# Storing less of a masked adjacency: turned parts only, byte masks for the rest

## The chip, the cores and the metric

The kernel runs on one core of a Trainium2 chip. The metric is device time in microseconds of one execution. It is written in Bass with the Tile framework, which sets the semaphores, hands out buffers and orders each engine's instructions. The engines are TensorE (PE, with its weight loads as PEld), VectorE (DVE), ScalarE (ACT), GpSimd (POOL) and SyncE (SP). SP, ACT and POOL issue DMAs.

## The reference

A batch holds 16 graphs of 1024 nodes with 128 features each. `adj` is a weighted adjacency with some 6% of its entries above zero. Its pattern is symmetric, its weights are not. Layer 0 is three graph convolutions, layer 1 a dilation of the adjacency and three more convolutions:

```python
def _sage(x, adj, Wr, Wx, b, mf):
    deg = jnp.clip(jnp.sum(adj, axis=-1, keepdims=True), 1.0, None)
    agg = jnp.einsum('bij,bjd->bid', adj, x) / deg
    out = agg @ Wr + x @ Wx + b
    nrm = jnp.maximum(jnp.linalg.norm(out, axis=-1, keepdims=True), NORM_EPS)
    return out / nrm * mf[..., None]
# layer 0: h = relu(layernorm(x)); three times h = (adj * cos(h W + b)) @ (h W + b); x = x + h
# layer 1: h = relu(layernorm(x))
adj_d = _dilate(adj, mask)          # keeps or drops entries, row after row
h1 = _bn(relu(_sage(h,  adj_d, Wr1, Wx1, b1, mf)), g1, be1)
h2 = _bn(relu(_sage(h1, adj_d, Wr2, Wx2, b2, mf)), g2, be2)
h3 = _bn(relu(_sage(h2, adj_d, Wr3, Wx3, b3, mf)), g3, be3)
xc = jnp.concatenate([h1, h2, h3], axis=-1) * mf[..., None]
return x + (xc @ Wl + bl) * mf[..., None]
```

`_bn` takes its statistics over all batches and nodes, so each convolution of layer 1 ends in a barrier over the 16 batches.

## The kernel before

All matrices are cut into blocks of 128 x 128, eight to a side (NCH = 8). Row q of a batch is handled as one tile of 2 x (8 - q) - 1 blocks: first the 8 - q blocks from the diagonal on, turned (transposed), then the 7 - q blocks of the mirrored column. For all q that makes 64 blocks a batch.

**Layer 0 and the dilation** share the first part. `layer0` is a generator: batches go in pairs, and `order` lists 48 rounds (six for a pair: three convolutions of two batches in turn). In a round, `products` forms cosines on PE and multiplies them into the adjacency on DVE, `turn` transposes, `sums` and `sums_back` accumulate, and line 387 evicts the round's sum into hTo. At fixed steps of a round, other work is placed: `fetch` loads x, `norm` is the layer norm (lines 135 to 150), `residual` and `next_layer` end a batch. Whether the next round is a batch's first is asked by `then.l == 0` and `after.l == 0`; `l` is raised in `sums_back`, three steps late. `adjT_tile` also transposes the adjacency and stores its upper blocks in `adjT_d` (line 242). The dilation runs between these pieces, by a planner's weights (`COLS`, `TURN`, `SPREAD`), mostly on DVE; it stores a 0/1 pattern `keep_d` in f16 (line 716).

**The second layer's first convolution** (block `c1`): `fetch` loads `kb`, the pattern of a batch, and `hN`. `masked(b, q, kb)` loads the turned blocks from `adjT_d` (line 920) and the others from `adj` (line 924) into slot aT{q}, transposes the pattern on PE (929), multiplies the two patterns into `both` (931), and masks the two parts of the slot (937 and 941). `turn` transposes the second part (954, 955) and stores the whole slot to `adT_d` (956, on POOL's queue). `follow`, two steps later (`LAG1`), runs `Sums.add`, whose matmuls (827) read the slot. A slot exists once for each q, so the next batch's loads wait for this batch's matmuls and for its store.

**The second and third convolution** (loop `for l in (1, 2)`): per batch eight loads `aT <- adT` (line 1043, on SP's queue), each followed by `add`. At q = 2 `start2` prepares the next batch: `normed` (1002), `weighted` (PE 799, ACT 800, DVE 801), and `project` (1012), which adds the projection of the previous convolution's output to `acc` (by ACT at 1020 or by DVE at 1022). In the third convolution `residual` loads x2 and adds bias and x2 to `acc` with 16 operations (1030 and 1034). `weigh` (856), `norms` (872, 876, and POOL at 877) and `keep` (165, 166, 887) end the sums. **The tail** projects the last output and adds `acc` (1068).

Tile orders instructions by priority, the order of the program, and moves ready ones into gaps that its model of the engines shows.

Of the kernel before, what the change touches and what calls it, by code (L numbers as in the profile page):

```python
# [7 lines left out]

F32 = mybir.dt.float32
F16 = mybir.dt.float16  # L10
I32 = mybir.dt.int32
AF = mybir.ActivationFunctionType
ALU = mybir.AluOpType
# [24 lines left out]
COLS, TURN = 0.215, 0.109  # L38

LAG1 = 2  # L40

SPREAD = 0.93
T_DIL = 10
# [3 lines left out]
def tile_adj_preln_d2(  # L47
# [49 lines left out]
    def base(q):  # L97


        return q * 2 * NCH - q * q  # L100

    dram = ctx.enter_context(tc.tile_pool(name="dram", bufs=1, space=DRAM))
    keep_d = [dram.tile([N, N], F16, tag=f"keep{b}", name=f"keep{b}") for b in range(B)]
    adT_d = [
        [
            dram.tile([P, base(q + 1) - base(q), P], F32, tag=f"adT{b}_{q}", name=f"adT{b}_{q}")
            for q in range(NCH)
        ]
        for b in range(B)
    ]  # L110
    adjT_d = [dram.tile([NCH, P, N], F32, tag=f"adjT{b}", name=f"adjT{b}") for b in range(B)]
    x2_d = [dram.tile([N, D], F32, tag=f"x2{b}", name=f"x2{b}") for b in range(B)]
    h0_d = [dram.tile([N, D], F32, tag=f"h0{b}", name=f"h0{b}") for b in range(B)]
# [55 lines left out]
    with ExitStack() as actx:  # L169
# [242 lines left out]
        batches = [Batch(b) for b in range(B)]  # L412
        order = [batches[b + i] for b in range(0, B, 2) for _ in range(3) for i in range(2)]

        def layer0():


# [24 lines left out]
            for i, now in enumerate(order + [None]):  # L442
# [5 lines left out]
                for s in range(NCH if now else LAG):  # L448
# [25 lines left out]
                    if ended:  # L474
# [4 lines left out]
                            yield NCH * TURN  # L479
                        if s == 5:  # L480
                            ended.next_layer()
                    if s == 5 and after and after.l == 0:
                        after.fetch()
                    if then:
                        new = then.l == 0
                        if s == 0 and new:
                            then.norm()
                        if s == 3 and new:
                            then.enter(0)
                            then.enter(1)  # L490
# [280 lines left out]
    with ExitStack() as bctx:  # L771
# [10 lines left out]
        def blocks_of(q, nm):  # L782


            return poolr.tile([P, 2 * (NCH - q) - 1, P], F32, tag=f"aT{q}", name=f"aT{q}_{nm}")

        def weighted(l, b, hT, ones):


            nm = f"{l}_{b}"  # L790
            hw = pool2.tile([P, NCH, P + ones], F32, tag="hw", name=f"hw_{nm}")
            if ones:
                nc.gpsimd.memset(hw[:, :, P:], 1.0)
            own = pool2.tile([P, NCH, D], F32, tag="own", name=f"own_{nm}")
            for h in range(NCH // 2):
                two = slice(2 * h, 2 * h + 2)
                pw = ps_sm.tile([P, 2, 2 * P], F32, tag="sm", name=f"pw_{nm}_{h}")
                for i in range(2):
                    nc.tensor.matmul(pw[:, i, :], lhsT=hT[:, 2 * h + i, :], rhs=wrx[:, l, :], start=True, stop=True)  # L799
                nc.scalar.activation(hw[:, two, :P], pw[:, :, :P], AF.Copy)  # L800
                nc.vector.tensor_tensor(  # L801
                    own[:, two, :], pw[:, :, P:], bs[:, l : l + 1, :].to_broadcast([P, 2, P]), ALU.add
                )
            return hw, own
# [84 lines left out]
        def batchnorm(l):  # L889

            mv = pool2.tile([P, 2], F32, tag="bn_mv", name=f"bn_mv_{l}")
            nc.vector.bn_aggr(mv, stats.rearrange("p s x -> p (s x)"))  # L892
            sd = pool2.tile([P, 1], F32, tag="bn_sd", name=f"bn_sd_{l}")
            nc.scalar.activation(sd, mv[:, 1:2], AF.Sqrt, bias=eps_col)
            nc.vector.reciprocal(sd, sd)
            ab = pool2.tile([P, 2], F32, tag="bn_ab", name=f"bn_ab_{l}")
            nc.vector.tensor_tensor(ab[:, 0:1], sd, gcol[:, l : l + 1], ALU.mult)
            mt = pool2.tile([P, 1], F32, tag="bn_mt", name=f"bn_mt_{l}")
            nc.vector.tensor_tensor(mt, mv[:, 0:1], ab[:, 0:1], ALU.mult)
            nc.vector.tensor_tensor(ab[:, 1:2], becol[:, l : l + 1], mt, ALU.subtract)  # L900
            return ab
# [2 lines left out]
        with ExitStack() as c1:  # L904
# [4 lines left out]
            def fetch(b):  # L909
                kb = poolk.tile([P, NCH, N], F16, tag="kb", name=f"kb_{b}")  # L910
                for c in range(NCH):
                    nc.sync.dma_start(kb[:, c, :], keep_d[b][c * P : (c + 1) * P, :])
                hN = pool2.tile([P, NCH, D], F32, tag="hN2", bufs=1, name=f"hN1_{b}")
                nc.scalar.dma_start(hN, h0_d[b].rearrange("(c p) d -> p c d", p=P))
                return kb, hN

            def masked(b, q, kb):
                row = NCH - q
                aT = blocks_of(q, f"1_{b}")
                nc.sync.dma_start(  # L920
# [6 lines left out]
                pk = ps_t.tile([P, NCH, P], F16, tag="pk", name=f"pkb_{b}_{q}")  # L927
                for c in range(row):
                    nc.tensor.transpose(pk[:, c, :], kb[:, q + c, q * P : (q + 1) * P], ident16)
                both = poolk.tile([P, NCH, P], F16, tag="both", name=f"both_{b}_{q}")  # L930
                nc.vector.tensor_tensor(
                    both[:, :row, :],
                    pk[:, :row, :],
                    kb[:, q, q * P :].rearrange("p (c q) -> p c q", q=P),
                    ALU.mult,
                )
                nc.vector.scalar_tensor_tensor(  # L937
                    aT[:, :row, :], aT[:, :row, :], 0.0, both[:, :row, :], ALU.max, ALU.mult
                )
                if row > 1:  # L940
                    nc.vector.scalar_tensor_tensor(
                        aT[:, row:, :], aT[:, row:, :], 0.0, both[:, 1:row, :], ALU.max, ALU.mult
# [3 lines left out]
            def turn(s, q, aT):  # L946

                b, row = s.b, NCH - q
                for c in range(1, row, CPH):
# [3 lines left out]
                    for i in range(n):  # L953
                        nc.tensor.transpose(pt[:, i, :], aT[:, at + i, :], ident)  # L954
                    nc.scalar.activation(aT[:, at : at + n, :], pt[:, :n, :], AF.Copy)  # L955
                nc.gpsimd.dma_start(adT_d[b][q], aT)

            last, behind = None, []

# [11 lines left out]
            for b in range(B):  # L971
                kb, hN = then
                hT = pool2.tile([P, NCH, P], F32, tag="hT2", name=f"hT1_{b}")
                transposed(ps_sm, hT, hN, f"h1{b}")
                now = Sums(0, b, hT, 3, 1, ps_a)
                for q in range(NCH):
                    behind.append((now, q, masked(b, q, kb)))
                    if len(behind) > 1:
                        turn(*behind[-2])
                    if len(behind) > LAG1:  # L980
# [3 lines left out]
                    if q == 4 and last is not None:  # L984
                        last.keep(0)
                        last.keep(1)
                        last = None
            turn(*behind[-1])
            while behind:
                follow()  # L990
# [4 lines left out]

        poolc = bctx.enter_context(tc.tile_pool(name="bc", bufs=1))
        ps_a = bctx.enter_context(tc.tile_pool(name="b_a2", bufs=2, space=PSUM))
        acc = poolc.tile([P, B, NCH, D], F32, name="acc")

        def normed(l, b, ab):  # L1000
            hT = pool2.tile([P, NCH, P], F32, tag="hT2", name=f"hT2_{l}_{b}")
# [5 lines left out]
        def project(l, b, hT):  # L1007

            for h in range(NHALF):
                pp = ps_sm.tile([P, CPH, P], F32, tag="sm", name=f"pp_{l}_{b}_{h}")  # L1010
                for c in range(CPH):
                    nc.tensor.matmul(pp[:, c, :], lhsT=hT[:, h * CPH + c, :], rhs=wl[:, l, :], start=True, stop=True)  # L1012
                yield h, pp, acc[:, b, h * CPH : (h + 1) * CPH, :]

        def start2(l, b):
            hT = normed(l, b, ab)
            got = Sums(l, b, hT, CPH, 0, ps_a)
            for h, pp, a in project(l - 1, b, hT):
                if l == 1:
                    nc.scalar.activation(a, pp, AF.Copy)  # L1020
                else:
                    nc.vector.tensor_tensor(a, pp, a, ALU.add)
            return got

        def residual(b):

            x2 = pool2.tile([P, NCH, D], F32, tag="hN2", bufs=1, name=f"x2f_{b}")
            nc.scalar.dma_start(x2, x2_d[b].rearrange("(c p) d -> p c d", p=P))
            for c in range(NCH):
                nc.vector.scalar_tensor_tensor(  # L1030
                    x2[:, c, :], blb[:, 0, :], mf[:, b, c : c + 1], x2[:, c, :], ALU.mult, ALU.add
                )
                a = acc[:, b, c, :]
                nc.vector.scalar_tensor_tensor(a, a, mf2[:, b, c : c + 1], x2[:, c, :], ALU.mult, ALU.add)

        for l in (1, 2):
            last = None
            then = start2(l, 0)
            for b in range(B):
                now = then  # L1040
                for q in range(NCH):
                    aT = blocks_of(q, f"{l + 1}_{b}")
                    nc.sync.dma_start(aT, adT_d[b][q])
                    now.add(q, aT)
                    if q == 1 and last is not None:
                        last.keep(0)
                    if q == 3 and last is not None:
                        last.keep(1)
                    if q == 2:
                        if b + 1 < B:  # L1050
                            then = start2(l, b + 1)
                        if l == 2:
                            residual(b)
                    if q == CPH - 1:
                        now.norms(0)
                    if q == NCH - 2 and b == B - 1:
                        now.keep(0)
                now.norms(1)
                last = now
            last.keep(1)  # L1060
            ab = batchnorm(l)

        for b in range(B):
            y = pool2.tile([P, NCH, D], F32, tag="o", name=f"y_{b}")
            for h, pp, a in project(2, b, normed(3, b, ab)):
                for c in range(CPH):
                    n = h * CPH + c
                    nc.vector.scalar_tensor_tensor(  # L1068
                        y[:, n, :], pp[:, c, :], mf2[:, b, n : n + 1], a[:, c, :], ALU.mult, ALU.add
                    )  # L1070
            nc.sync.dma_start(out[b].rearrange("(c p) d -> p c d", p=P), y)


# [48 lines left out]
```

## Time and profile before

| what | us |
|---|---|
| median of 3 runs | 2987.47 |
| lowest and highest | 2986.51, 2990.78 |
| the profiled execution | 2990.07 |
| its span, first to last instruction | 2988.3 |
| PE, PEld, DVE busy in it | 2699.3, 2228.7, 1974.3 |
| ACT, POOL busy in it | 1468.3, 449.3 |

The mean granted clock of TensorE is 0.967. The DMA queues moved 593.67 MB, 199 GB/s on average. "Busy" is time in which an engine worked on an instruction; waits, semaphores and the issuing of DMAs by SP are not in it. Matmuls overlap, so a busy PE is not PE at its peak. "DMA share" is the mean busy share of the core's 16 DMA engines. A wait is put down to whatever ended last before the waiting instruction began.

The stages lie in the span thus: layer 0 with the dilation up to about 1748 us, then the first convolution of the second layer up to 2252, the second up to 2592, the third up to 2932, and the tail.

### The profile page before, as it was taken

How to read it: one execution, taken by the hardware profiler on the slowest of the kernel's cores; microseconds unless marked ns; L12 is line 12 of the kernel's file. 1: busy time of each engine (PE TensorE's matmuls, PEld its weight loads, DVE VectorE, ACT ScalarE, POOL GpSimd, SP SyncE). 2: the span in 40 equal slices, each digit the busy share in tenths (PEclk: the TensorE clock that was granted, in tenths of full speed). 3: DMA queues.
4: the chain of work that ended last, by engine and by line, in shares of the span. 5: the costliest groups of instructions: out<-in, count | busy, mean ns of one | idle time of the engine just before them, and what ended most of it. 6: DMA issues, size and time to landing. Idle time of an engine off the chain costs nothing. (4 is left out here: it accounts for less than half of the span.)

```text
span 2988.3 us, 52459 instructions
## 1 busy us (share of the span) xinstructions
PE 2699.3 (90%) x18803; PEld 2228.7 (75%) x18803; DVE 1974.3 (66%) x5233; ACT 1468.3 (49%) x4213; POOL 449.3 (15%) x604
## 2 busy tenths in 40 slices
PE   5999898998989889998999979988898999899996
PEld 3666676666666666666666668888888999899995
DVE  2878778878878788778877446666662333366555
ACT  5867657657546556566455223333333343333333
POOL 2112012011111111121111012212121101010110
PEclk9999999999999999999999989999999999999998
DMA  8446347346356476296351079999995566566763
GB/s 265 157 137 210 109 153 236 91 158 198 103 171 174 116 218 178 80 262 171 89 176 64 3 262 375 361 351 360 361 322 213 195 206 218 177 227 228 246 213 113
DMA packets 399664, 593.67 MB, mean 199 GB/s; under 512 B 85456, under 2 KB 283984, under 8 KB 399392
## 3 DMA queue, kind: packets, MB, share of 16 engines
q1 hardware_dynamic: 326640, 416.89, 44.6%
q0 software_dynamic: 38464, 156.07, 14.4%
q10 hardware_dynamic: 34288, 17.24, 2.0%
q8 instruction: 152, 2.49, 0.3%
q14 instruction: 120, 0.98, 0.1%
HBM read 411.83 MB, written 163.58 MB: 193 GB/s over the span
## 5 line engine op out<-in xcount | busy, mean ns | idle before, releaser
L827 PE MATMUL agg<-hw,aT 128*128 128x128 f32 (+1 forms) x6144 | 754.8, 280 | 9.1 <-DVE aT L937 8.0
L827 PEld LDWEIGHTS agg<-hw,aT 128*128 128x128 f32 x6144 | 726.7, 196 | 13.8 <-DVE aT L937 11.0
L324 PE MATMUL pg<-nhT 128*128 128x512 f32 (+3 forms) x1152 | 459.3, 501 | 64.7 <-DVE ew L336 59.1
L364 PE MATMUL po<-ew,hS 128*128 128x512 f32 (+3 forms) x1152 | 459.5, 502 | 12.5 <-ACT hTo L387 8.5
L336 DVE TENSOR_TENSOR ew<-pg,adjA 128x768 f32<-128x768 f32 (+3 forms) x528 | 423.7, 824 | 4.4 <-DVEq L764 2.9
L378 PE MATMUL po<-ew,hS 128*128 128x128 f32 x2688 | 365.3, 276 | 0.0
L378 PEld LDWEIGHTS po<-ew,hS 128*128 128x128 f32 x2688 | 337.8, 193 | 35.4 <-issue 34.8
L354 ACT ACTIVATE ew<-gt 128x512 f32<-128x512 f32 (+1 forms) x480 | 208.6, 464 | 219.5 <-PE gt L353 216.2
L324 PEld LDWEIGHTS pg<-nhT 128*128 128x128 f32 x1152 | 189.1, 194 | 162.4 <-issue 110.9
L695 DVE TENSOR_TENSOR_SCAN rank<-patt 128x1024 f16<-128x1024 f16 x128 | 292.4, 2294 | 0.7
L364 PEld LDWEIGHTS po<-ew,hS 128*128 128x128 f32 x1152 | 197.2, 195 | 106.2 <-issue 74.6
L353 PEld LDWEIGHTS gt<-ident,ew 128*128 128x128 f32 x1344 | 168.2, 143 | 102.7 <-issue 70.3
L333 DVE TENSOR_TENSOR ew<-pg,adjA 128x128 f32<-128x128 f32 x384 | 106.5, 277 | 170.5 <-PE pg L324 137.8
L353 PE MATMUL gt<-ident,ew 128*128 128x128 f32 x1344 | 211.9, 277 | 5.8 <-ACT ew L354 4.5
L801 DVE TENSOR_TENSOR own<-pw,bs 128x256 f32<-128x256 f32 x192 | 78.8, 423 | 201.7 <-ACT hw L800 201.7
L877 POOL TENSOR_TENSOR o<-o,rn 128x512 f32<-128x512 f32 x96 | 103.9, 1082 | 668.6 <-DVE rn L876 423.7
L799 PE MATMUL pw<-wrx,hT 128*128 128x256 f32 x768 | 181.1, 390 | 10.4 <-ACT hT L1002 9.7
L955 ACT ACTIVATE aT<-pta 128x512 f32<-128x512 f32 (+3 forms) x160 | 70.5, 468 | 216.6 <-PE pta L954 193.5
L856 DVE SCALAR_TENSOR_TENSOR o<-agg,invdeg,own 128x128 f32<-128x128 f32 x384 | 111.5, 343 | 96.4 <-PE agg L827 87.3
L799 PEld LDWEIGHTS pw<-wrx,hT 128*128 128x128 f32 x768 | 146.2, 195 | 33.1 <-ACT hT L1002 10.5
L800 ACT ACTIVATE hw<-pw 128x256 f32<-128x256 f32 x192 | 70.6, 384 | 202.2 <-PE pw L799 149.0
L872 ACT ACTIVATE own<-o 128x128 f32<-128x128 f32 x384 | 115.3, 303 | 96.6 <-DVE o L856 96.6
(161 smaller groups left out, 4101.8 us busy)
## 6 DMA issues: line engine op xcount, KB each, us to landing
an<-in_adj_dram SPq DMA_DIRECT2D x128, 512.0 KB, 4.8
keep<-kp POOLq DMA_DIRECT2D x128, 256.0 KB, 3.6
kb<-keep SPq DMA_DIRECT2D x128, 256.0 KB, 5.7
aT<-adT SPq DMA_DIRECT2D x32, 960.0 KB, 4.7
aT<-adT SPq DMA_DIRECT2D x32, 832.0 KB, 4.6
xb<-in_x_dram SPq DMA_DIRECT2D x47, 512.0 KB, 4.6
aT<-adT SPq DMA_DIRECT2D x32, 704.0 KB, 4.1
aT<-adT SPq DMA_DIRECT2D x32, 576.0 KB, 3.4
```

Of the source, the lines that this page charges most:

```text
L324: nc.tensor.matmul(pg[:, :n, :].rearrange("p c q -> p (c q)"), lhsT=self.nhT[:, q * P : (q + 1) * P], rhs=self.nhT[:, (q + c) * P : (q + c ...
L333: nc.vector.tensor_tensor(ew[:, 0, :], pg[:, 0, :], place[:, 0, :], ALU.mult)
L336: nc.vector.tensor_tensor(both[0][:, :, off, :], pg[:, own:n, :].unsqueeze(1).to_broadcast([P, 2, n - own, P]), both[1][:, :, off, :], ALU ...
L353: nc.tensor.transpose(pt[:, i, :], ew[:, at + i, :], ident)
L354: nc.scalar.activation(ew[:, at : at + n, :], pt[:, :n, :], AF.Copy)
L364: nc.tensor.matmul(self.po[:, c * P : (c + n) * P], lhsT=self.hS[:, q, :], rhs=ew[:, c - q : c - q + n, :].rearrange("p c q -> p (c q)"), ...
L378: nc.tensor.matmul(self.po[:, q * P : (q + 1) * P], lhsT=self.hS[:, q + n, :], rhs=ew[:, NCH - 1 - q + n, :], start=False, stop=closes and ...
L695: nc.vector.tensor_tensor_scan(rank, pt[:, 1 : N + 1], pt[:, 2:], 0.0, ALU.add, ALU.add)
L799: nc.tensor.matmul(pw[:, i, :], lhsT=hT[:, 2 * h + i, :], rhs=wrx[:, l, :], start=True, stop=True)
L827: nc.tensor.matmul(self.place(c), lhsT=aT[:, blk, :], rhs=self.hw[:, source, :], start=source == 0 and c % self.ga == 0, stop=ends(c, source),
L856: nc.vector.scalar_tensor_tensor(self.o[:, c, :], self.place(c)[:, :P], invdeg[:, b, c : c + 1], self.own[:, c, :], ALU.mult, ALU.add,)
L872: nc.scalar.activation(self.own[:, n, :], self.o[:, n, :], AF.Square, accum_out=ss[:, c : c + 1])
```

## The change

In the first convolution the slot's first part (turned adjacency, masked) is no longer stored; only the second part is. The product of the patterns is written as bytes into a tile `masks` of 36 blocks for the whole batch, and stored once a batch to `mask_d`. In the second and third convolution each slot is filled by two loads, the first part from `adjT_d` (not masked) and the second from `adT_d`, six products ahead (`AHEAD`); the masks come in two pieces a batch (q from 0 to 3, and from 4). DVE masks the first part again (`unmasked`), three products ahead (`MASKED`). The sum `acc` is one tile for each batch; x2 is loaded into it at the start, two batches ahead in the second convolution, each projection is multiplied by the squared node mask and added to it, and `bias` adds the bias in the third. In layer 0 the two questions after `l == 0` become a question after the round's number (`first`), so that `fetch` and `norm` run once for a batch; before, they also ran in the first two rounds of a pair.

```diff
+AHEAD, MASKED = 6, 3
...
-            dram.tile([P, base(q + 1) - base(q), P], F32, tag=f"adT{b}_{q}", name=f"adT{b}_{q}")
-            for q in range(NCH)
+            dram.tile([P, NCH - 1 - q, P], F32, tag=f"adT{b}_{q}", name=f"adT{b}_{q}")
+            for q in range(NCH - 1)
...
+    mask_d = [dram.tile([P, NMASK, P], U8, tag=f"mask{b}", name=f"mask{b}") for b in range(B)]
...
+        def first(i):
+
+            return i % 6 < 2
...
-                    if s == 5 and after and after.l == 0:
+                    if s == 5 and after and first(i + 2):
                         after.fetch()
                     if then:
-                        new = then.l == 0
+                        new = first(i + 1)
...
+        def unmasked(aT, q, mask):
+
+            here = aT[:, : NCH - q, :]
+            nc.vector.scalar_tensor_tensor(here, here, 0.0, mask, ALU.max, ALU.mult)
...
-                both = poolk.tile([P, NCH, P], F16, tag="both", name=f"both_{b}_{q}")
+                both = masks[:, mbase(q) : mbase(q + 1), :]
                 nc.vector.tensor_tensor(
-                    both[:, :row, :],
+                    both,
...
-                nc.vector.scalar_tensor_tensor(
-                    aT[:, :row, :], aT[:, :row, :], 0.0, both[:, :row, :], ALU.max, ALU.mult
-                )
+                unmasked(aT, q, both)
...
-                nc.gpsimd.dma_start(adT_d[b][q], aT)
+                if row > 1:
+                    nc.gpsimd.dma_start(adT_d[b][q], aT[:, row:, :])
...
+                masks = poolk.tile([P, NMASK, P], U8, tag="masks", name=f"masks_{b}")
...
+                nc.gpsimd.dma_start(mask_d[b], masks)
...
-        acc = poolc.tile([P, B, NCH, D], F32, name="acc")
+        acc = [poolc.tile([P, NCH, D], F32, name=f"acc{b}") for b in range(B)]
...
+        def projected(l, b, hT, dst):
+
+            for h, pp in project(l, b, hT):
+                for c in range(CPH):
+                    n = h * CPH + c
+                    nc.vector.scalar_tensor_tensor(
+                        dst[:, n, :], pp[:, c, :], mf2[:, b, n : n + 1], acc[b][:, n, :], ALU.mult, ALU.add
+                    )
...
         def residual(b):
 
-            x2 = pool2.tile([P, NCH, D], F32, tag="hN2", bufs=1, name=f"x2f_{b}")
-            nc.scalar.dma_start(x2, x2_d[b].rearrange("(c p) d -> p c d", p=P))
+            nc.scalar.dma_start(acc[b], x2_d[b].rearrange("(c p) d -> p c d", p=P))
+
+        def bias(b):
             for c in range(NCH):
...
+                a = acc[b][:, c, :]
+                nc.vector.scalar_tensor_tensor(a, blb[:, 0, :], mf[:, b, c : c + 1], a, ALU.mult, ALU.add)
+
+
+        MASKS = (0, CPH, NCH)
+        rows, mask_of = {}, {}
+
+        def load(l, b, q):
+            row = NCH - q
+            rows[l, b, q] = aT = blocks_of(q, f"{l + 1}_{b}")
+            if q in MASKS:
+                i = MASKS.index(q)
+                m0, m1 = mbase(q), mbase(MASKS[i + 1])
+                mask_of[l, b, i] = m = poolc.tile([P, m1 - m0, P], U8, tag=f"m{i}", bufs=1 + i, name=f"m{i}_{l}_{b}")
+                nc.sync.dma_start(m, mask_d[b][:, m0:m1, :])
+            nc.sync.dma_start(aT[:, :row, :].rearrange("p c q -> p (c q)"), adjT_d[b][q][:, q * P :])
+            if row > 1:
+                nc.sync.dma_start(aT[:, row:, :], adT_d[b][q])
+
+        def mask(l, b, q):
+            i = q >= CPH
+            m0 = mbase(MASKS[i])
+            unmasked(rows[l, b, q], q, mask_of[l, b, i][:, mbase(q) - m0 : mbase(q + 1) - m0, :])
+
+        steps = [(l, b, q) for l in (1, 2) for b in range(B) for q in range(NCH)]
+        for b in range(2):
+            residual(b)
+        for s in steps[:AHEAD]:
+            load(*s)
+        for s in steps[:MASKED]:
+            mask(*s)
...
+            if at + AHEAD < len(steps):
+                load(*steps[at + AHEAD])
+            if at + MASKED < len(steps):
+                mask(*steps[at + MASKED])
+            now.add(q, rows.pop((l, b, q)))
...
+            if q == 2:
+                if b + 1 < B:
+                    then = start2(l, b + 1)
+                if l == 2:
+                    bias(b)
...
+            if q == 4 and l == 1 and b + 2 < B:
+                residual(b + 2)
```

More of the change, by code (lines that the diff above doesn't have):

```diff
@@ L10 @@
 F16 = mybir.dt.float16
+U8 = mybir.dt.uint8
 I32 = mybir.dt.int32
@@ L100, in base, with mbase @@
         return q * 2 * NCH - q * q
+    def mbase(q):
+        return q * NCH - q * (q - 1) // 2
     dram = ctx.enter_context(tc.tile_pool(name="dram", bufs=1, space=DRAM))
@@ L110, in tile_adj_preln_d2 @@
     ]
+    NMASK = NCH * (NCH + 1) // 2
+    mask_d = [dram.tile([P, NMASK, P], U8, tag=f"mask{b}", name=f"mask{b}") for b in range(B)]
     adjT_d = [dram.tile([NCH, P, N], F32, tag=f"adjT{b}", name=f"adjT{b}") for b in range(B)]
@@ L892, in batchnorm @@
             nc.vector.bn_aggr(mv, stats.rearrange("p s x -> p (s x)"))
-            sd = pool2.tile([P, 1], F32, tag="bn_sd", name=f"bn_sd_{l}")
+            sd = pool2.tile([P, 1], F32, tag="bn_sd", bufs=1, name=f"bn_sd_{l}")
             nc.scalar.activation(sd, mv[:, 1:2], AF.Sqrt, bias=eps_col)
@@ L897, in batchnorm @@
             nc.vector.tensor_tensor(ab[:, 0:1], sd, gcol[:, l : l + 1], ALU.mult)
-            mt = pool2.tile([P, 1], F32, tag="bn_mt", name=f"bn_mt_{l}")
+            mt = pool2.tile([P, 1], F32, tag="bn_mt", bufs=1, name=f"bn_mt_{l}")
             nc.vector.tensor_tensor(mt, mv[:, 0:1], ab[:, 0:1], ALU.mult)
@@ L912, in fetch, with masked @@
                     nc.sync.dma_start(kb[:, c, :], keep_d[b][c * P : (c + 1) * P, :])
-                hN = pool2.tile([P, NCH, D], F32, tag="hN2", bufs=1, name=f"hN1_{b}")
+                hN = poolk.tile([P, NCH, D], F32, tag="hN2", bufs=1, name=f"hN1_{b}")
                 nc.scalar.dma_start(hN, h0_d[b].rearrange("(c p) d -> p c d", p=P))
                 return kb, hN
-            def masked(b, q, kb):
+            def masked(b, q, kb, masks):
                 row = NCH - q
@@ L975, in tile_adj_preln_d2 @@
                 now = Sums(0, b, hT, 3, 1, ps_a)
+                masks = poolk.tile([P, NMASK, P], U8, tag="masks", name=f"masks_{b}")
                 for q in range(NCH):
-                    behind.append((now, q, masked(b, q, kb)))
+                    behind.append((now, q, masked(b, q, kb, masks)))
                     if len(behind) > 1:
@@ L1012, in project @@
                     nc.tensor.matmul(pp[:, c, :], lhsT=hT[:, h * CPH + c, :], rhs=wl[:, l, :], start=True, stop=True)
-                yield h, pp, acc[:, b, h * CPH : (h + 1) * CPH, :]
+                yield h, pp
+        def projected(l, b, hT, dst):
[5 more added lines that the diff above has]
+                    )
         def start2(l, b):
@@ L1017, in start2 @@
             got = Sums(l, b, hT, CPH, 0, ps_a)
[L1018 to L1022, printed above, removed]
+            projected(l - 1, b, hT, acc[b])
             return got
         def residual(b):
-            x2 = pool2.tile([P, NCH, D], F32, tag="hN2", bufs=1, name=f"x2f_{b}")
-            nc.scalar.dma_start(x2, x2_d[b].rearrange("(c p) d -> p c d", p=P))
+            nc.scalar.dma_start(acc[b], x2_d[b].rearrange("(c p) d -> p c d", p=P))
@@ L1029, in residual @@
+        def bias(b):
             for c in range(NCH):
[L1030 to L1039, printed above, removed]
-                now = then
[L1041 to L1057, printed above, removed]
@@ new lines, in mask @@
+        def mask(l, b, q):
[9 more added lines that the diff above has]
+            mask(*s)
+        now = None
+        for at, (l, b, q) in enumerate(steps):
+            if q == 0:
+                if b == 0:
+                    last, then = None, start2(l, 0)
+                now = then
+            if at + AHEAD < len(steps):
[3 more added lines that the diff above has]
+            now.add(q, rows.pop((l, b, q)))
+            if q == 1 and last is not None:
+                last.keep(0)
+            if q == 2:
[3 more added lines that the diff above has]
+                    bias(b)
+            if q == 3 and last is not None:
+                last.keep(1)
+            if q == CPH - 1:
+                now.norms(0)
+            if q == 4 and l == 1 and b + 2 < B:
+                residual(b + 2)
+            if q == NCH - 2 and b == B - 1:
+                now.keep(0)
+            if q == NCH - 1:
@@ L1058, in tile_adj_preln_d2 @@
                 now.norms(1)
                 last = now
-            last.keep(1)
-            ab = batchnorm(l)
+                if b == B - 1:
+                    last.keep(1)
+                    ab = batchnorm(l)
         for b in range(B):
             y = pool2.tile([P, NCH, D], F32, tag="o", name=f"y_{b}")
[L1065 to L1070, printed above, removed]
+            projected(2, b, normed(3, b, ab), y)
```

## The prediction

> **What bounds the kernel now.** I read the page's first line, then the table of stretches (cut where the code's stages start: layer 0 with the dilation, the second layer's first convolution, its second, its third, the tail), and then each stretch's own waits. Columns of the table: stretch, length, busy time and instructions of PE, PEld, DVE, ACT and POOL, granted clock, DMA share, GB/s.
>
> ```profile
> span 2988.3 us, 52459 instructions
> ...
> 0.00:1748.00 1748.00, 1561.68 (x9609) 1135.43 (x9610) 1325.05 (x3380) 1045.70 (x2791) 274.25 (x366) 0.98 0.52 152
> 1748.00:2252.00 504.00, 440.56 (x3563) 416.12 (x3561) 317.00 (x791) 165.15 (x572) 108.10 (x174) 0.92 0.97 358
> 2252.00:2592.00 340.00, 330.61 (x2688) 322.40 (x2688) 102.95 (x325) 126.98 (x433) 33.26 (x32) 0.98 0.59 200
> 2592.00:2932.00 340.00, 329.41 (x2688) 321.52 (x2688) 193.85 (x607) 110.47 (x401) 33.73 (x32) 0.98 0.62 209
> 2932.00:2988.30 56.30, 37.09 (x256) 33.25 (x256) 35.44 (x133) 20.04 (x17) 0.00 (x0) 0.86 0.48 150
> ```
>
> Four regimes. In the first convolution (504 us, 31.5 us for each of 16 batches) the DMA engines are at 0.97. In the second and third (340 us each) PE is at 97% and DMA at 0.6. In layer 0 PE is busiest, at 89%, with DVE at 76%. The waits of SP's queue in the first convolution name the load that suffers (queue, line, waited for, us in total, times, longest):
>
> ```profile
> SPq L920 <- DMA adT<-aT: 143.2, 63, 6.7
> ```
>
> L920 loads the turned blocks into slot aT{q}; the slot is free only when the whole of it, stored by L956, has landed. So 143 of 504 us SP, and every load behind it, stands still for that store. The chain of waits in the second convolution (start, length, what) shows the other regime:
>
> ```profile
> 2394.44 3.46 PE pw L799 x16
> 2397.89 1.78 PE pp L1012 x16
> 2399.68 2.01 PE agg L827 x18
> ...
> 2402.12 9.83 PE agg L827 x88
> ...
> 2412.39 2.46 PE agg L827 x22
> 2414.84 3.46 PE pw L799 x16
> ```
>
> From pw to pw are 20.4 us, PE without a gap. No transfer matters there; loads wait for PE, not PE for loads.
>
> **What the skill says.** "DMA: Bandwidth & Descriptors", section "Issuing engines are not separate DMA queues": DMAs from any issuer share the same 16 engines. The trace agrees: POOL's stores and SP's loads together make the 0.97. So stored bytes that go away leave room for loads. "VectorE: DVE Perf Modes", section "The perf-mode tier table": a two-tensor operation on f32 yields one element a cycle. No SCALAR_TENSOR_TENSOR with a byte operand is in the trace; L937, f32 with an f16 mask, takes 1212 ns for 1024 elements and 292 for 128. "SBUF — State Buffer", section "SBUF: two separate sides": a DVE operation with two SBUF inputs and a GpSimd operation that reads SBUF exclude each other for a whole instruction. The timeline of the third convolution agrees: four L1030 beside an L877 take 1.94 us, where five L1034 without one took 1.39.
>
> ```profile
> 2698.75 1.39 DVE L1034 SCALAR_TENSOR_TENSOR acc<-acc,mf,x2f 128x128 f32<-128x128 f32 x5
> ...
> 2708.78 1.94 DVE L1030 SCALAR_TENSOR_TENSOR x2f<-blb,mf,x2f 128x128 f32<-128x128 f32 x4
> ```
>
> ```profile
> 2709.01 1.04 POOL L877 TENSOR_TENSOR o<-o,rn 128x512 f32<-128x512 f32 x1 [2.99 <-DVE rn L876]
> ```
>
> **The change, part by part.** The groups that price it (busy us, mean ns | idle before):
>
> ```profile
> L148 ACT ACTIVATE h<-xb,ln_nmr_l,ln_rstd_l 128x128 f32<-128x128 f32 x256 | 106.9, 489 | 14.3 <-DVE ln_nmr_l L146 13.1 <-issue 0.9
> L937 DVE SCALAR_TENSOR_TENSOR aT<-aT,both 128x1024 f32<-128x1024 f32 (+7 forms) x128 | 96.0, 750 | 9.9 <-DMA aT<-adjT 7.9
> L1030 DVE SCALAR_TENSOR_TENSOR x2f<-blb,mf,x2f 128x128 f32<-128x128 f32 x128 | 50.3, 438 | 38.4 <-DMA x2f<-x 38.4
> ```
>
> *Stores of the first convolution.* 64 blocks of 64 KB a batch become 28, plus 36 byte blocks of 16 KB: 4.19 MB become 1.84 + 0.59, so 16 batches save 28.3 MB. The stretch moved 358 GB/s x 504 us = 180 MB in 0.97 x 504 = 489 us of engine time, 2.71 us per MB: 77 us go, 412 stay. At a share of 0.97 that is a stretch of 425 us. PE's own work there, from spacings in its timeline (agg 0.112 us, pw 0.216, f32 transposes 0.109, f16 0.056): 128 x 0.112 + 16 x 0.216 + 44 x 0.109 + 36 x 0.056 = 24.6 us a batch, 394 in all. DVE keeps its 317. With DMA (26 us a batch) and PE (25) now nearly equal and engines that issue in order, neither will be full: I take 450 us (DMA 0.92, PE 0.88), a gain of 54. Bounds: 425 (gain 79) and 475 (gain 29, if the slot's round through load, mask, two steps of lag and store sets the pace). L931 writes bytes in place of f16; one element a cycle either way, 55.8 us in all, so nothing (+-5 on DVE, which has room). The mask store is one more issue on POOL's queue a batch; POOL is busy 21%. Its two buffers are free a whole batch ahead.
>
> *Second and third convolution: DMA and queues.* Loads go from 4.19 to 2.36 + 1.84 + 0.59 = 4.79 MB a batch, 14% more, and from 8 issues on SP to 17. At 209 GB/s and 0.62 that makes a share near 0.7: hidden behind PE, which frees each slot a batch ahead. The first mask piece has one buffer; its last reader, the mask of q = 3, is queued two products before the next batch's load of it, so SP is not held. x2 moves from a transfer in the third convolution to one in the second on ACT's queue, two batches ahead; DVE waited 38.4 us for it (L1030) without PE noticing.
>
> *The masks on DVE.* 96.0 / 16 = 6.0 us more a batch. In the second convolution DVE has 102.95 / 16 = 6.4; masks and eight L1068-like operations in place of ACT's two evictions of 0.60 us (8 x 0.29 = 2.3, four at a time take 1.14 in the tail) make 14.7 of 20.4. In the third: 12.1 now; out go L1030 (46.9/16 = 2.9), L1034 (2.4) and L1022 (1.4), in come masks 6.0, projections 2.3, bias 2.9: 16.6, and with about one more wait for POOL's port in each of two L877, 18. PE's first aT wait cannot be hidden if a mask is late: behind it in PE's queue stand all later products. Masks are queued three products ahead, but the last three products of a batch take only 2.0 us (9 blocks), and in DVE's queue the next batch's first mask (1.21 us) stands behind own, projection, bias and the weighing of four chunks. DVE's gaps (own waited 58.7 us for ACT's hw in that stretch) give room for a mask to go earlier. I take +2 us for the second and +6 for the third convolution; bounds 0 and +15, 0 and +40. Below nothing is excluded: PE has no gaps to fill.
>
> *Norms once.* L148 runs 256 times where 16 batches need 128. Out go 16 norms, each 8 x (0.27 + 0.16) + 0.4 = 3.8 us on DVE and 8 x 0.49 + 0.3 = 4.2 on ACT, and 16 fetches of x on SP. On what path? Layer 0 works a pair of batches off in six rounds; the starts of hTo (L387) in the trace give each round's length. Means of six pairs by place in the six: 38.3, 32.5, 33.6, 32.1, 35.0, 41.8 us. The repeated norms run in the first two places, but the second is no longer than the third, which has none; the first and last also hold transposes of the next adjacency. So PE's work covers most: I take 0.5 us for each, -8 us. Bounds: -25 (DVE in turn with PE sets the pace) and +12 (another interleaving of the same work). Tail: the same 128 operations, 0; loads before the second convolution: under 2 us.
>
> **Sum.** -54 + 2 + 6 - 8 = -54. The profiled execution took 2990.07 us (span 2988.3 and 1.8 around it), so 2936; it stands 2.6 above the median of 2987.47, so **2934** by the median.
>
> **Rivals.** *Latency, not bandwidth* (20%): slots and SP's order keep the first convolution near 475-490 us, and the second and third give back some. For it: the wait L920 is for a landing, not for bandwidth alone. Against: 0.97 share. 2960-2981. *More than counted* (13%): the floor of 425 is reached and layer 0 gains its 25: 2987 - 79 - 25 + 5 = 2888. *Slower: DVE becomes the bound of the convolutions* (9%): a late mask holds PE each batch. The gain of 62 is spent when the 32 batches cost 1.9 us more each, 22.3 in place of 20.4. With strict program order in the third convolution, the first mask comes about 2 us late, and with port waits on each 1.2 us mask, 4; with 1.5 in the second: 16 x 5.5 = 88, so 3013. Against: DVE's sum stays under 20.4. *It doesn't do what it says* (under 1%): counts of stores would stay.
>
> **Numbers.** The likeliest case has 58% and lies within 2910-2960. A measurement of this kernel tells 0.2% (6 us) from no change. Faster: 58 + 13 + most of the 20 = 0.87; same 0.04; slower 0.09. The range leaves out half of the best case and the slower one: 2892 to 2978.
>
> **What would show it.** After: the first convolution near 450 us, DMA share a little over 0.9, PE busier, L920's wait for adT well under 143 us; the second and third still 340-346, DVE near 75% and 85-90%, no PE wait for a masked aT over some us; L148 x128. A first convolution above 480, or PE waits for the mask of q = 0 in every batch, would prove me wrong.

## Result: 1% slower, and the profile after

The changed kernel takes 3019.24 us (median of 4 runs, 3016.77 to 3022.97) against 2989.12 for the kernel before on the same occasions: ratio 1.0102, 95% interval 1.0084 to 1.0119. The forecast was 2934, within 2892 to 2978; it was wrong in size and in sign.

The profiled span (3018.2 us) is cut here where the stages start in the trace: at the first transpose of the pattern (pkb), and at the three aggregations of the statistics (bn_mv). The table of stretches of the changed kernel has the same columns as the prediction's:

```profile
0.00:1741.40 1741.40, 1547.61 (x9588) 1125.15 (x9588) 1294.12 (x3090) 993.71 (x2642) 274.18 (x366) 0.98 0.50 148
1741.40:2233.70 492.30, 434.04 (x3584) 410.77 (x3584) 357.18 (x787) 168.27 (x576) 108.73 (x174) 0.94 0.93 312
2233.70:2598.30 364.60, 336.37 (x2688) 323.06 (x2688) 229.58 (x587) 109.27 (x401) 33.94 (x32) 0.97 0.73 233
2598.30:2961.40 363.10, 334.71 (x2688) 321.20 (x2688) 256.21 (x701) 109.55 (x401) 38.99 (x32) 0.98 0.61 197
2961.40:3018.20 56.80, 38.69 (x256) 35.62 (x256) 36.05 (x133) 20.04 (x17) 0.00 (x0) 0.83 0.47 148
```

The kernel before, cut at the same events, has 1752.9, 498.9, 340.4, 339.1 and 57.0. (The prediction's window of 504 us for the first convolution began some 5 us before it.) So layer 0 gained 11.5 us, the first convolution only 6.6 where 54 were forecast, and the second and third lost 24.2 and 24.0 where 2 and 6 were allowed. With 0.2 us from the tail the sum is 29.9, the difference of the spans.

Two things stand out. DVE's busy time in the first convolution rose from 316 to 357 us, and DMA moved only 312 GB/s at a share of 0.93. In the later convolutions DVE is far from full (63% and 71%), and still PE lost its gapless rhythm. The waits of both later convolutions together (engine, line, waited for, us in total, times, longest), first DVE's, then PE's:

```profile
DVE aT L804 <- DMA aT<-adjT: 168.1, 160, 7.7
```

```profile
PE pw L818 <- DVE own L820: 34.2, 28, 3.9
PE pw L818 <- ACT hT L1022: 14.1, 2, 9.2
```

DVE stands still 168 us before the second masking (L804), because the load is not there; PE does not wait for the masked blocks at all but for `own`, which empties PE's PSUM tiles. The chain of waits shows one turn of a ring that repeats in each batch (start, length, what):

```profile
2312.22 9.83 PE agg L846 x88
...
2322.07 4.63 DMA aT<-adjT
...
2326.79 1.09 DVE aT L804
2327.88 0.35 DVE own L820
...
2328.27 1.13 PE pw L818 x4
2329.41 1.78 PE pp L1032 x16
2331.19 2.01 PE agg L846 x18
2333.20 0.44 PE pt_r L175 x4
2333.64 9.83 PE agg L846 x88
```

PE frees a slot; only then can the next batch's block be loaded (4.6 us); DVE masks it (1.09) and only after that comes to `own` (0.35), for which PE waits. This turn takes 21.4 us against 20.4 in the kernel before; in the third convolution the same chain takes about 22. DVE's own timeline shows the order in its queue:

```profile
2410.52 1.23 DVE L804 SCALAR_TENSOR_TENSOR aT<-aT,m 128x1024 f32<-128x1024 f32 x1 [3.51 <-DMA aT<-adjT]
2411.66 0.69 DVE L906 BATCH_NORM_STATS2 stats<-hR 128x6 f32<-128x512 f32 x1
2412.81 1.09 DVE L804 SCALAR_TENSOR_TENSOR aT<-aT,m 128x896 f32<-128x896 f32 x1 [0.46 <-DMA aT<-adjT]
2413.82 1.08 DVE L820 TENSOR_TENSOR own<-pw,bs 128x256 f32<-128x256 f32 x3
```

The masks of 1024 and 896 elements belong to q = 0 and q = 1 of the next batch. The program writes them at q = 5 and 6 of the present one. They stand in the queue before the `own` that the program writes at q = 2, so Tile has moved them ahead, presumably because its model took them for ready there.

In the first convolution one group explains the rise of DVE. The groups of one shape, of the kernel before and of the changed one:

```profile
L931 DVE TENSOR_TENSOR both<-pkb,kb 128x1024 f16<-128x1024 f16 x16 | 10.9, 679 | 9.5 <-DMA aT<-adjT 9.5
```

```profile
L950 DVE TENSOR_TENSOR masks<-pkb,kb 128x1024 uint8<-128x1024 f16 x16 | 19.5, 1217 | 0.6 <-DMA aT<-adjT 0.4 <-DMA mask<-masks 0.2
```

With a byte output the product takes 1217 ns in place of 679. PE feels it, because its next transposes of the pattern go into a tile that the product has to read first:

```profile
PE pkb L948 <- DVE masks L950: 32.1, 30, 3.1
```

And the second convolution has a fault of its own at its start, which ACT's queue shows (ACTq is the issuing of DMAs):

```profile
2247.36 12.68 ACTq L1052 DMA_DIRECT2D acc<-x  x4
2260.14 0.38 ACT L819 ACTIVATE hw<-pw 128x256 f32<-128x256 f32 x1 [11.56 <-DMA acc<-x]
```

The program writes the loads of x2 two batches ahead, but all sixteen were issued at the front, between 2226 and 2261 us; an eviction hw waited 11.6 us behind their issues.

### The profile page after: what moved, and what is told of

The parts are those of the page before. It is cut to its first block, busy times and chain, and to the rows that moved or that the text cites. A ratio compares the mean times of both kernels' runs of the same rounds, so it can differ in the third digit from the quotient of the medians.

```text
span 3018.2 us, 52657 instructions
## 1 busy us (share of the span) xinstructions
PE 2691.4 (89%) x18803; PEld 2215.8 (73%) x18803; DVE 2173.2 (72%) x5297; ACT 1400.8 (46%) x4037; POOL 455.8 (15%) x604
## 4 chain that ended last, share of the span: by engine, by line
PE 51%; DVE 20%; DMA 15%; issue 8%; ACT 4%; POOL 1%; SPq 0%; POOLq 0%; DVEq 0%; ACTq 0%; another core or an unknown queue 0%
PE agg L846 18%; PE po L374 7%; PE pg L334 6%; DMA aT<-adjT 6%; DVE rank L709 5%; PE po L388 5%; DVE ew L346 4%; PE gt L363 3%; PE pw L818 2%; PE pp L1032 2%; DVE aT L804 2%; DMA kl<-keep 2%; PE pw L283 2%; PE pta L971 1%; DVE patt L564 1%
## 5 line engine op out<-in xcount | busy, mean ns | idle before, releaser
L804 DVE SCALAR_TENSOR_TENSOR aT<-aT,m 128x1024 f32<-128x1024 f32 (+7 forms) x256 | 204.6, 805 | 182.9 <-DMA aT<-adjT 168.1
L818 PE MATMUL pw<-wrx,hT 128*128 128x256 f32 x768 | 191.1, 398 | 48.7 <-DVE own L820 34.2
L896 POOL TENSOR_TENSOR o<-o,rn 128x512 f32<-128x512 f32 x96 | 110.2, 1148 | 721.6 <-DVE rn L895 715.1
L311 POOL TENSOR_TENSOR hS<-hN,rn 128x1024 f32<-128x1024 f32 x48 | 94.6, 1970 | 410.5 <-DVE rn L167 302.3
```

The costliest lines, as they stand in the source:

```text
L804: nc.vector.scalar_tensor_tensor(here, here, 0.0, mask, ALU.max, ALU.mult)
L896: nc.gpsimd.tensor_tensor(self.o[:, hc, :], self.o[:, hc, :], rn.unsqueeze(2).to_broadcast([P, CPH, D]), ALU.mult)
```

## The experiments

Each time is a median, with the ratio to the kernel before and its interval. Stage times are from one trace of each run, cut as above. They carry some spread: in the four runs that change nothing but the later convolutions, the first convolution takes 481.6 to 490.6 us where the changed kernel has 492.3.

**The masks' place in DVE's queue.** One call pins an instruction behind everything that the program traced before it on its engine.

```diff
...
-            unmasked(rows[l, b, q], q, mask_of[l, b, i][:, mbase(q) - m0 : mbase(q + 1) - m0, :])
+            tc.keep_in_program_order(
+                unmasked(rows[l, b, q], q, mask_of[l, b, i][:, mbase(q) - m0 : mbase(q + 1) - m0, :])
+            )
```

> The changed kernel with one edit: in the second and third convolution each second masking is pinned behind what the program traces before it on DVE (three products ahead as written), so that it can't be queued ahead of the weights' own part (L820) of the next batch. Theory A (order in DVE's queue: a mask that waits for a load stands ahead of own, and PE waits for own): the two loops fall from 363 us each to about 340-345, total about 2975. Theory B (transfers: 14% more bytes and twice the loads): they stay near 363, total 3019. Theory C (DVE has too much work beside POOL's port): they stay near 363 or grow, and in the third more than in the second. If masks in written order come late, as my rival of the prediction had it, PE waits for aT at q = 0 and the third loop is above 345.

3066.07 us, 1.0275 (1.0248 to 1.0301): slower still, by 6.6 us in the second and 53 in the third convolution (371.2 and 416.2). DVE's wait for loads was gone (0.3 us between 2260 and 2925), so the order was what made DVE wait; but the written order is too late. The names of the waits were not as expected: PE waited for `o` of POOL (L896), 27.0 us in the second and 53.2 in the third, and hardly for aT (0.6). POOL's timeline:

```profile
2721.15 3.94 POOL L896 TENSOR_TENSOR o<-o,rn 128x512 f32<-128x512 f32 x1 [17.37 <-DVE rn L895]
```

At 2720.90 DVE begins four masks back to back, 3.29 us, and the multiplication on POOL, 1.04 us in the kernel before, lasts 3.94 and ends 0.9 us after the last of them; the transposes of keep wait for it. The third convolution shows this length in 14 of its batches. It fits the exclusion of DVE operations with two SBUF inputs and GpSimd reads, which the prediction took from the Trainium skill, with DVE as the one that keeps POOL out. The next batch's first masks run in the same gap of PE, so the run does not tell how much of it the masks' lateness alone would have cost.

```diff
-AHEAD, MASKED = 6, 3
+AHEAD, MASKED = 6, 5
```

With this edit too:

> As the run before, but the masks are written five products ahead in place of three, so that the next batch's first mask comes right behind own and the projection of q = 2. Theory A: 340-342 us for each loop, total about 2970, no PE wait for a mask. Theory B and C: near 363, total 3019.

2969.36 us, 0.9949 (0.9931 to 0.9967). The third convolution takes 341.6 us, the second 349.3. The same masks, loads and DVE work, in another order, cost 2.5 us in the third where they had cost 24. Theories B and C fall there. POOL is still held up (its 32 multiplications in the third take 77 us in place of 34), but PE waits for it 4.9 us only: the collision costs where PE needs `o` at once. Five products ahead without the pin was not tried.

> The changed kernel without the second masking: the first part of each slot is used unmasked in the second and third convolution (this part of the computation is left out); all loads stay, those of the byte masks too. Theory A and C: both loops at 340, total about 2973. Theory B: both stay near 363, total 3019.

```diff
...
-            if at + MASKED < len(steps):
-                mask(*steps[at + MASKED])
```

2975.95 us, 0.9965 (0.9953 to 0.9977): the third convolution 340.1, the second 356.5. Loads in two parts cost nothing in the third. On the byte masks this run says less than was meant: with nothing reading them, all their loads were issued by 2406.5 us, in the second convolution, so the third had 15 issues a batch and no more bytes than before. The kernel with the masks five products ahead loads them all, 17 issues and 14% more bytes a batch, and takes 341.6 us. Without masks the second still lost 16 us, nearly all at its start (PE waits 17.9 us in its first 38); x2 loads and sixteen mask loads in a row (27.3 us on SP) stand there together.

**The ring opened in another way.** The masks stay unpinned and early, but the loads need not wait for PE:

```diff
...
-            return poolr.tile([P, 2 * (NCH - q) - 1, P], F32, tag=f"aT{q}", name=f"aT{q}_{nm}")
+            return poolr.tile(
+                [P, 2 * (NCH - q) - 1, P], F32, tag=f"aT{q}", bufs=2 if q in (0, 1, 2) else 1, name=f"aT{q}_{nm}"
+            )
...
```

> The changed kernel with a second slot for each of aT0, aT1 and aT2; to make room, acc has 11 tiles that the 16 batches share (so the projected sums of five batches are mixed with others': that part of the computation is changed). In DVE's queue the next batch's first three masks still stand ahead of own, unpinned, but their loads no longer wait for PE to free the slot. Theory A in its full form (PE frees the slot, load, mask, own, PE: a ring that takes longer than PE's 20.4 us of work): the ring is open, the third convolution falls from 363 us to 340-345, the second to about 350 (x2 loads at its start stay). If it were the masks' own time ahead of own (3.1 us of DVE work) that delays PE, both stay above 355. The first convolution gets second slots too: if the round through the slots set its pace, it falls below 480; if the byte product on DVE does, it stays at 487-492.

2967.67 us, 0.9948 (0.9930 to 0.9966). The three later stretches of that kernel:

```profile
1735.80:2233.20 497.40, 437.00 (x3584) 413.77 (x3584) 357.27 (x787) 169.17 (x576) 108.48 (x174) 0.94 0.92 315
2233.20:2577.40 344.20, 330.47 (x2688) 321.87 (x2688) 235.82 (x591) 109.68 (x401) 33.94 (x32) 0.98 0.75 246
2577.40:2917.10 339.70, 330.01 (x2688) 321.97 (x2688) 259.48 (x700) 109.58 (x401) 34.65 (x32) 0.98 0.61 203
```

Masks ahead of `own` do no harm once their loads are early: in the third convolution three masks still stand right before it (at 2635.15 us, 3.10 long), and it takes 339.7 us with 259 us of DVE work. So it was the wait behind a slot that PE had to free, not the masks' time. The second is a less clean test, since the shared acc tiles also spread the x2 loads, up to 2323 us. The first convolution, with second slots for q = 0 to 2 too, stayed at 497: there the round through these slots was not what held the time.

**The x2 loads.**

```diff
-            nc.scalar.dma_start(acc[b], x2_d[b].rearrange("(c p) d -> p c d", p=P))
+            tc.keep_in_program_order(nc.scalar.dma_start(acc[b], x2_d[b].rearrange("(c p) d -> p c d", p=P)))
```

> The kernel of e2_pin5 with one more edit: the loads of x2 into acc (L1052) are pinned in ACT's queue behind what the program traces before them, so that the sixteen of them are not issued all at the start of the second convolution. Theory F (at that start ACT's queue stands still behind these issues, first for the landing of the last byte-mask store, then for room in the queue, and hw and own wait behind it): the second convolution falls from 349 us to 340-342, total about 2960. Rival G (the second convolution is longer because its first masks and loads come late): it stays at 349, total 2969.

2959.93 us, 0.9916 (0.9896 to 0.9937); the second convolution takes 340.7 in place of 349.3, the third 340.1, with all loads and masks. Each x2 load now takes at most 0.6 us to issue, where the changed kernel has up to 7.3. Theory F holds as to where the time went; that the queue had no room was not shown.

**The byte product.** First with the byte tile filled by POOL:

> The changed kernel with the product of the patterns in the first convolution written in f16 again (as before the change) and used for the masking there; the byte tile is set to ones by POOL and stored as in the changed kernel, so the second masking of the later convolutions multiplies by ones (that part of the computation is left out). Same transfers, DVE work of the first convolution back by 40 us. Theory D (the byte product on DVE holds PE at each batch's start): the first convolution falls from 492 us to 470-480, total about 3003. Theory E (the loads' and stores' round through the slots sets its pace): 490 or so, total 3017. The later loops stay at 363.

2990.03 us, 1.0012 (1.0000 to 1.0023); the first convolution 471.2, the later ones as expected at 366.6 and 363.4. Theory D holds, but the run probably understates it: POOL, which fills the tile, was busy 168 us there in place of 109, and DVE's own time fell only to 330. So ACT makes the byte copy instead, in the changed kernel:

```diff
-                both = masks[:, mbase(q) : mbase(q + 1), :]
+                both = poolk.tile([P, NCH, P], F16, tag="both", name=f"both_{b}_{q}")[:, :row, :]
...
+                nc.scalar.activation(masks[:, mbase(q) : mbase(q + 1), :], both, AF.Copy)
                 unmasked(aT, q, both)
```

> The changed kernel with one edit alone: the product of the patterns in f16 on DVE and its byte copy made by ACT; the computation is whole. If the byte product's price is independent of the other two faults, the first convolution falls from 492 us to about 460, the later loops stay at 363 each, total about 2988, about as fast as the kernel before. If ACT's copies only helped because the other edits were there, it stays above 475.

2977.38 us, 0.9973 (0.9961 to 0.9985): the first convolution 457.0, 35 us less than in the changed kernel, and PE's wait for the product fell from 32.1 to 6.2 us. (The kernel before has 35.4 us of that wait too, but with half the store and an f16 product it is 2.9, in the next run.) The later ones are 367.8 and 359.3, so the fault of the masks' order is independent of it.

**The parts that were meant to gain, alone.** The store, in the kernel before:

```diff
...
-                nc.gpsimd.dma_start(adT_d[b][q], aT)
+                if row > 1:
+                    nc.gpsimd.dma_start(adT_d[b][q], aT[:, row:, :])
...
-                    nc.sync.dma_start(aT, adT_d[b][q])
+                    row = NCH - q
+                    nc.sync.dma_start(aT[:, :row, :].rearrange("p c q -> p (c q)"), adjT_d[b][q][:, q * P :])
+                    if row > 1:
+                        nc.sync.dma_start(aT[:, row:, :], adT_d[b][q])
```

> The kernel before with the store of the first convolution cut to the slot's second part and the loads of the later convolutions in two parts (first part from the turned adjacency, unmasked: this part of the computation is left out), no byte masks anywhere, norms twice as before. Theory H (my prediction's step: 2.71 us of engine time per MB): stores fall by 37.7 MB, 102 us of engine time, PE at 394 becomes the bound, the first convolution falls from 499 us to 420-440. Theory E (the round of load, mask, matmul and store through a slot, and queue order, set its pace): 460-475. The later convolutions: 340 each if twice the loads cost nothing (theory A), above 350 if they do (theory B).

2926.71 us, 0.9800 (0.9776 to 0.9823). The first convolution takes 439.3 us, at the upper end of theory H; the later ones 339.3 and 340.3.

```profile
1749.50:2188.80 439.30, 414.51 (x3560) 391.29 (x3560) 317.07 (x788) 165.79 (x570) 100.09 (x158) 0.98 0.93 323
```

> The kernel before with only the norms and the loads of x done once for a batch. My prediction's step: layer 0 shorter by 8 us, total 2978; DVE in turn with PE: by 25, total 2961; nothing: 2986.

2975.98 us, 0.9967 (0.9953 to 0.9981): 6 to 14 us of gain by the interval, as the step said. In its trace nearly 19 us less up to the first transpose of the pattern (1734.2), 3 more in the first convolution.

**All mended** (five products ahead, both pins, ACT's byte copy; whole computation):

> The kernel of e7_pin5_x2 with the product of the patterns in f16 again and a byte copy of it made by ACT (36 blocks a batch, about 6 us more on ACT, which is busy a third of the first convolution); the computation is whole. If DVE's byte product is what cost the first convolution, it falls from 487 us to about 472 and the total to about 2943; if ACT's copies come in the way of its evictions (hw, aT), it stays at 480 or more.

2931.95 us, 0.9822 (0.9802 to 0.9841), faster than both kernels, by 1.8% and 2.8% (0.9822 / 1.0102). Its three convolutions and PE's wait for the product:

```profile
1734.20:2185.30 451.10, 421.05 (x3584) 398.39 (x3584) 316.58 (x784) 243.89 (x704) 104.37 (x174) 0.98 0.96 335
2185.30:2529.30 344.00, 330.64 (x2688) 322.50 (x2688) 249.75 (x586) 109.42 (x401) 47.36 (x32) 0.98 0.76 254
2529.30:2869.80 340.50, 330.72 (x2688) 321.69 (x2688) 259.63 (x705) 109.53 (x401) 77.69 (x32) 0.98 0.65 210
```

```profile
PE pkb L948 <- DVE both L950: 6.4, 7, 1.6
```

With DVE's busy time back at 317 us, DMA carries 335 GB/s at 0.96, and the first convolution is 48 us shorter than in the kernel before (451.1 for 498.9), where the prediction had 54 for the change as it was. The 472 expected for this run were drawn from the one with POOL's fill.

## Why the prediction was wrong, step by step

*Stores of the first convolution: right in mechanism, undone by another step.* On the cut of the result, where the kernel before has 498.9 us, a gain of 54 means 445; the runs have 451 with the byte masks' store (the mended kernel) and 439 without it, gains of 48 and 60. One term of the working was off: engine time per MB is no constant. It was 0.98 / 0.359 = 2.73 us per MB before and 0.93 / 0.323 = 2.88 with half the stores, so about 5% of the engine time came back. Why a byte takes longer in that mix was not tried. The sign that the prediction named, a wait of L920 for adT well under 143 us, hardly came even where the gain did: 116 us in the changed kernel, 114 with half the store and 111 in the mended one. That wait did not tell the length of the stage. And the granted clock of the stage rose, from 0.92 in the kernel before to 0.98 in both these runs; what part of the gain is the clock's was not separated.

*"One element a cycle either way, so nothing": the first step that failed.* The byte product cost 357 - 317 = 40 us of DVE time and, by the run with ACT's copy, 35 us of the first convolution (492 to 457); with the other faults mended 30 (481.6 to 451.1). The row was before my eyes: 679 ns is little over half of L937's 1212 for the same 1024 elements a partition, so it went through the elements about twice as fast. The Trainium skill says it too ("VectorE: DVE Perf Modes", section "What auto-detection actually checks"): the packed mode needs every tensor to be 16 bits wide, the output among them. The trace agrees, with 679 and 1217. I read the price of L937 onto an operation that ran in another mode, and "DVE has room" does not excuse it in a stretch where PE's next transposes wait for the product (32.1 us, then 6.2).

*"DVE's gaps give room for a mask to go earlier": the second.* I saw that Tile moves ready work forward and counted it as help. It is help only if the work is ready on the chip when it is reached. That PE frees each slot a batch ahead, as the forecast says, is early enough for PE's next use of it, but not for a mask that stands before `own`. The load waits for the slot, so an early mask holds the queue, and `own` behind it holds PE. That cost 15 us in the second and 22 in the third convolution (364.6 to 349.3, 363.1 to 341.6). The forecast named what stands behind a late mask in PE's queue and did not ask who stands behind an early one in DVE's. The third's 24 us lie inside its bound of +40, the second's 24 outside +15.

*x2 "two batches ahead, hidden": the third.* Its issues went to the front of ACT's queue: 8.6 us (349.3 to 340.7).

*Right:* loads in two parts cost nothing in the third convolution (340.1, without the masking and with everything in the run with both pins); DVE's sum stayed below PE's (256 of 363, in the mended kernel 260 of 340.5); norms once gained 10 us by the ratio of its own run for 8 forecast, though layer 0 alone reads 11.5 in the changed kernel's trace and 18.7 in two others.

*The rivals.* The slower one had 9%, and its 3013 us are near the 3019 measured, but by luck: no mask was late for PE, DVE was no bound, and most of the first convolution's gain, which it kept, was lost. In written order masks are late indeed (3066), and PE's wait is then for POOL's multiplication, not for aT. "Latency, not bandwidth" falls with the mended kernel: its slots are single, and its first convolution takes 451 us, not 475 to 490.

The changed kernel in terms of the forecast: 2934, plus 47 in the first convolution (a gain of 7 for 54), plus 40 in the later ones (a loss of 48 for 8), less 3.5 in layer 0, make 3018 of the 3019 measured. The three failed steps, by their own runs 35, 37 (15 + 22) and 9 us, account for 81 us of the difference of 85.

## What to carry to other kernels

An instruction that a scheduler may move forward is priced by what stands behind it in its engine's queue: if its input comes through a buffer that the bound engine must free first, pin it behind the work that this engine needs, or give the buffer a second copy. Before costing a changed type at nothing, compare the time per element in the operation's own row with that of a like operation; if it shows a packed mode, ask whether each operand, the output included, still allows it. And test the parts of a compound change alone: here a gain of some 53 us (that of the mended kernel) and three faults of about 80 us came out as 30 us of loss.

## What the runs showed of the hardware

- A product of two f16 operands (one in PSUM) into f16 takes 679 ns for 128 x 1024, into bytes 1217. As an input of the f32 masking, bytes cost the same as f16: 1216 and 1212 ns.
- In the first convolution a DMA share of 0.98 carried 359 GB/s in the kernel before, 0.96 carried 335 in the mended one and 0.93 carried 312 in the changed one: 2.73, 2.87 and 2.98 us of engine time per MB. The share alone did not tell how many bytes fit.
- A GpSimd multiplication of 1.04 us lasted 3.94 us in 14 batches of the third convolution in written order; in the one shown it ran beside 3.29 us of back-to-back DVE operations with two SBUF inputs.
- DMAs issued in a row on ACT's queue (L1052) took up to 7.3 us each to issue and held the engine's own work for up to 11.6 us; spread over the stage each took at most 0.6 us.
